# A written sequence for the closing part of a perceiver block

## The chip, the core and the metric

The kernel runs on one core of a Trainium2 chip. The core has five instruction queues: TensorE (PE, with its weight loads as PEld), VectorE (DVE), ScalarE (ACT), GpSimd (POOL) and SyncE (SP, which here only issues DMAs). Each queue runs in order, and the queues wait for each other by semaphores. The metric is the device time of one execution in microseconds (us); less is better.

## What is computed

16 items, each with x of 128 x 512 and a context of 2048 x 512, all in float32. Three stages, each added to its input, each behind a layernorm:

```python
x = x + softmax(ln(x) @ ctx.T) @ ctx                      # cross attention
q, k, v = heads of ln(x) through W*_down and W*_up        # 16 heads of 32, rotary halves
x = x + (softmax(causal(q @ k.T * scale)) @ v) @ Wc       # self attention
h = ln(x); g = softmax over the top 2 of (h[row 0] @ Wr.T)
x = x + h + sum over the two chosen experts e of g[e] * ((h @ A[e].T) @ Bw[e].T)
```

Which experts an item uses is known only when the first row of its own h is; their weights are then gathered from DRAM by index.

## The kernel before, in words

Python generators hold the stages of one item, and `step(kind, b, n)` runs n parts of a generator: `score` (L265: context scores and their softmax), `attend` (L328: the weighted context, matmuls av in four quarters, and the layernorm 2), `inner` (L350: q, k, v, heads, output projection o, and layernorm 3) and `experts` (L650: routing, the two experts' matmuls mid and ffn, result and store). The weights are folded first; then a loop (L760) takes items 0 to 13, one round each, in which item b runs `inner`, b - 1 runs `experts`, b + 1 `attend`, b + 2 `score`. From L808 on stands the closing part for items 13 (only its experts), 14 (called y) and 15 (called z), which have no later item to run beside.

The sequence of instructions comes from the compiler's scheduler, which may change the order on an engine, except between instructions that were given to `tc.keep_in_program_order` (called `pinned`, L112): these keep the order in which the program names them. All matmuls and transposes are pinned (L99, L102); on DVE and POOL only a few are, on ACT almost none.

A tile from a pool lies in a room that goes by its tag; a pool with bufs=1 has one room per tag, and a new tile in it waits until all readers of the old one are done. PSUM has eight banks: three for `ps_tr`, two for `ps_sc`, three for `ps_acc`.

Parts that the prediction follows:

- `layernorm` (L128): statistics on DVE (L132, L134), the root on POOL (L136, L139), the normalising pass on DVE (L142).
- `transposed` (L169): for most items by DVE blocks and two DMAs; where `by_tensor` holds (items 0, 1 and the last ones) by four PE transposes and an ACT copy (L178).
- `weigh` (L437): for each group of four heads a masked add (L441), a maximum (L447), four exponentials on ACT (L449), a reciprocal and a multiplication (L453, L454).
- `route` (L562): one matmul lg, seven small DVE operations, two indirect gathers into `each` (L581), one into `wb` (L586), and a POOL copy from `each` into `wa` (L591). `each` has one room.
- `early` (L608): for item 15 the first row alone is carried through v, output projection, layernorm and routing ahead of the others, so that its experts are known sooner: matmuls v0, v0t, o0 (by `padded`, L635), o0t, tr_row, with copies on DVE (L627, L635).
- `experts`: mid (L666), its scaling by the gate on ACT (L671), the residual sum `res` (L674, L676), ffn (L683), the result (L684) and the store (L685), on POOL's queue except for item 15. `res` has one room.

## Time and profile before

| | us |
|---|---|
| three runs | 838.35, 835.94, 838.13; median 838.13 |
| the profiled execution | 836.97 |
| span of its records | 835.2 |
| matmuls of item 14's first head scores begin (closing part) | 752.69 |
| last matmul ends | 829.34 |
| last DVE instruction ends | 831.50 |
| the two last stores are issued | 831.19 and 831.9 |

The page sums the busy time of each engine and cuts the span into 40 slices. A line of stretches gives, after its bounds and length, the busy time and count of PE, PEld, DVE, ACT and POOL, then the granted TensorE clock (1.00 is full), the DMA share and GB/s. A line of waits gives who stood, for whom, the sum, how often and the longest. A line of the chain gives start, length, engine and tile. The names there are those of the program: h for a layernorm's result, rs for its root, res for the residual sum, each, wa and wb for the experts' weights.

### The profile page before, as it was taken

The numbers are of one execution on the slowest core, as the hardware profiler recorded it, in microseconds if no ns is written. First come the engines' busy times: TensorE is split into PE (matmuls) and PEld (weight loads), VectorE is DVE, ScalarE is ACT, GpSimd is POOL, SyncE is SP. The second block draws the span as 40 slices with busy tenths as digits, with TensorE's granted clock in tenths as the row PEclk, the third lists the DMA queues.
The fourth block names the chain that finished last, engine by engine and source line by source line (L and its number), as shares of the span: only waits on it lengthen the run. The fifth ranks groups of instructions, "written<-read, shape, count | busy, mean of one in ns | idle before, by whom it ended". The sixth has DMA issues, their size and how long they took to land.

```text
span 835.2 us, 14284 instructions
## 1 busy us (share of the span) xinstructions
PE 804.6 (96%) x5500; PEld 569.6 (68%) x5500; DVE 529.9 (63%) x1234; ACT 258.9 (31%) x766; POOL 146.1 (17%) x215
## 2 busy tenths in 40 slices
PE   6999999999999999999999999999999999997974
PEld 6846675768677676868667576867757686864733
DVE  1454759386675849577585948667593956657652
ACT  1223324142232415133332424223241512324331
POOL 1001001212121111212111121212111121212013
PEclk9999999999999999999999999999999999999878
DMA  9998294968849495876949496785949578551002
GB/s 368 396 349 340 90 369 172 345 248 273 335 163 414 147 357 218 300 301 204 398 143 381 174 332 271 248 345 182 386 159 352 218 276 329 177 214 38 1 20 69
DMA packets 76739, 211.04 MB, mean 253 GB/s; under 512 B 6400, under 2 KB 42624, under 8 KB 60288
## 3 DMA queue, kind: packets, MB, share of 16 engines
q10 hardware_dynamic: 15696, 113.32, 33.9%
q1 hardware_dynamic: 56880, 84.23, 28.7%
q0 software_dynamic: 4096, 12.59, 4.6%
q8 instruction: 43, 0.70, 0.3%
q14 instruction: 24, 0.20, 0.1%
HBM read 180.23 MB, written 29.88 MB: 252 GB/s over the span
## 4 chain that ended last, share of the span: by engine, by line
PE 89%; DVE 5%; POOL 2%; ACT 1%; issue 1%; DMA 1%; DVEq 0%; POOLq 0%; ACTq 0%
PE psc L100 28%; PE av L100 25%; PE v L100 7%; PE o L100 6%; PE k L100 6%; PE q L100 6%; PE y L100 2%; PE pss_sc L100 2%; PE pss_acc L100 1%; PE mid L100 1%; PE ffn L100 1%; ACT att L449 1%; DMA each<-in_A_dram,g_blocks 1%; PE lg L100 0%; PE tr_m L103 0%
## 5 line engine op out<-in xcount | busy, mean ns | idle before, releaser
L100 PE MATMUL psc<-hT,ctxT 128*128 128x128 f32 x2048 | 237.3, 277 | 1.4 <-ACT hT L178 1.4
L100 PEld LDWEIGHTS psc<-hT,ctxT 128*128 128x128 f32 x2048 | 233.3, 193 | 2.5 <-ACT hT L178 2.0
L100 PE MATMUL av<-ctx,sc 128*128 128x512 f32 x512 | 227.1, 595 | 0.0
L100 PEld LDWEIGHTS av<-ctx,sc 128*128 128x128 f32 x512 | 94.5, 190 | 111.0 <-issue 108.8
L449 ACT ACTIVATE att<-att,nmx 128x128 f32<-128x128 f32 x256 | 98.7, 387 | 91.4 <-DVE nmx L447 91.4
L136 POOL TENSOR_SCALAR rs<-mv 128x1 f32<-128x1 f32 x48 | 10.8, 225 | 410.2 <-DVE g_at L575 209.3
L287 ACT COPY sc<-psc 128x512 f32<-128x512 f32 x64 | 37.5, 586 | 140.1 <-PE psc L100 140.1
L315 ACT ACTIVATE sc<-sc 128x512 f32<-128x512 f32 x64 | 40.2, 630 | 90.9 <-DVE sc L312 90.4
L100 PE MATMUL v<-w_v,hT 128*32 128x512 f32 x520 | 60.5, 605 | 0.9 <-DVE w_v L234 0.9
L100 PE MATMUL k<-hT,w_k 128*128 128x128 f32 x512 | 60.9, 277 | 0.0
L100 PE MATMUL o<-w_c,yT 128*128 128x512 f32 x128 | 59.7, 609 | 0.5 <-ACT yT L493 0.5
L100 PEld LDWEIGHTS k<-hT,w_k 128*128 128x128 f32 x512 | 59.3, 194 | 1.2 <-issue 1.2
L100 PE MATMUL q<-hT,w_q 128*128 128x128 f32 x512 | 60.0, 275 | 0.0
L100 PEld LDWEIGHTS q<-hT,w_q 128*128 128x128 f32 x512 | 58.5, 192 | 0.3 <-issue 0.3
L290 DVE TENSOR_TENSOR mx<-psc,mx 128x512 f32<-128x512 f32 x32 | 21.6, 676 | 55.6 <-ACT sc L287 55.6
L142 DVE TENSOR_SCALAR h<-x,mv,rs 128x512 f32<-128x512 f32 x48 | 28.2, 587 | 37.3 <-POOL rs L139 37.3
L415 ACT ACTIVATE kb<-kT,cst 128x512 f32<-128x512 f32 (+1 forms) x34 | 36.2, 1111 | 43.0 <-DVE kT L403 43.0
L449 ACT ACTIVATION_READ_ACCUMULATOR att<-att,nmx 128x1 f32 x256 | 47.8, 187 | 0.0
L312 DVE TENSOR_TENSOR sc<-sc,spread 128x512 f32<-128x512 f32 x64 | 42.6, 672 | 3.3 <-PE spread L100 3.3
L454 DVE TENSOR_TENSOR att<-att,rsm 128x512 f32<-128x512 f32 x64 | 43.3, 677 | 0.7
L447 DVE TENSOR_REDUCE nmx<-att 128x4 f32<-128x512 f32 x64 | 41.6, 672 | 0.0
L290 DVE TENSOR_TENSOR mx<-psc,sc 128x512 f32<-128x512 f32 x16 | 11.1, 691 | 47.2 <-ACT sc L287 47.2
(134 smaller groups left out, 855.4 us busy)
## 6 DMA issues: line engine op xcount, KB each, us to landing
ctx<-in_ctx_dram ACTq DMA_DIRECT2D x56, 1024.0 KB, 8.9
ctxT<-in_ctxT_dram ACTq DMA_DIRECT2D x52, 1024.0 KB, 10.6
there_p<-pX SPq DMA_DIRECT2D x28, 512.0 KB, 4.0
pT<-there_p SPq DMA_DIRECT2D x28, 512.0 KB, 4.5
ctxT<-in_ctxT_dram SPq DMA_DIRECT2D x12, 1024.0 KB, 8.0
there<-blocks SPq DMA_DIRECT2D x42, 256.0 KB, 3.3
hT<-there SPq DMA_DIRECT2D x42, 256.0 KB, 3.0
ctx<-in_ctx_dram SPq DMA_DIRECT2D x8, 1024.0 KB, 9.2
```

The costliest lines, as they stand in the source:

```text
L100: tc.keep_in_program_order(nc.tensor.matmul(*args, **kwargs))
L136: eps = nc.gpsimd.tensor_scalar_add(rstd, mv[:, 1:2], EPS)
L142: place(nc.vector.tensor_scalar(to, of, mv[:, 0:1], rstd, ALU.subtract, ALU.mult))
L287: nc.scalar.copy(sc[:, v], ps)
L290: nc.vector.tensor_tensor(mx, ps, mx if v > 1 else sc[:, 0], ALU.max)
L312: nc.vector.tensor_tensor(sc[:, v], sc[:, v], spread[:, None, :S].to_broadcast([P, 4, S]), ALU.add)
L315: nc.scalar.activation(sc[:, v], sc[:, v], AF.Exp)
L415: nc.scalar.activation(kb[:, chunks, half, :].rearrange("p c (q i) -> p c q i", q=4), kT[:, chunks, :].rearrange("p c (i q) -> p c q i" if ...
L447: nc.vector.tensor_reduce(nmx[:, hs], att[:, hs, :], AX.X, ALU.max, negate=True)
L449: nc.scalar.activation(att[:, i, :], att[:, i, :], AF.Exp, bias=nmx[:, i : i + 1], accum_out=sm[:, i : i + 1],)
L454: nc.vector.tensor_tensor(att[:, hs, :], att[:, hs, :], rsm[:, hs, None].to_broadcast([P, 4, S]), ALU.mult)
```

## The change

The closing part from the second quarter of `attend` for item 15 on is cut into some 150 named pieces, and a text lists them in the order in which they are issued. A name is the piece and its item: m0.14 is the masked add of head group 0 of item 14, mx the maximum, e the exponentials, n the normalising; av, den, rden, x1 are the end of `attend`; st, mv, rs, h (2, 3 or r for the row) the layernorm; tr, hT transposes and copy; k, q with S, P, C, A the four rotary steps and kb the blocked copy; pss the head scores; tp, pT transposes and copies of the probabilities; v, vv, y, yT, o, x2 the rest of `inner`; share, lg, choose, ga, gb, wa, ex, gate the routing; mid, midT, f, rx, r the experts; v0, v0s, v0t, pad, row_o, o0s, o0t, row, trr the early row.

The list as far as the second layernorm of item 15, and its end:

```diff
+CLOSING = """
+pss0.14 av1.15 m1.14 m0.14 share.13 mx1.14 rx.13 e1.14 lg.13 fold.15 av2.15 choose.13 mx0.14
+ga.13 last_fold.15 e0.14 n1.14 den.15 av3.15 ex.13 n0.14 gb.13 rden.15 gate.13 wa.13 pss1.14
+x1.15 tp0.14 st2.15 mv2.15 mid.13 m2.14 rs2.15 pT0.14 h2.15 midT.13 mx2.14 tr2.15 f.13 m3.14
+hT2.15 e2.14 k0.15 r.13 mx3.14 n2.14 e3.14 q0.15 k0S.15 k0P.15 n3.14 k1.15 q0S.15 q0C.15
+k0C.15 k0A.15 q1.15 k1C.15 kb0.15 k1S.15 k1P.15 k1A.15 tp1.14 q1C.15 kb1.15 q0P.15 v0.15
+q0A.15 pT1.14 q1S.15 pss0.15 q1P.15 v0s.15 q1A.15 v0t.15 m1.15 mx1.15 pss1.15 pad.15 m0.15
+e1.15 y.14 mx0.15 row_o.15 m2.15 yT.14 n1.15 e0.15 o.14 mx2.15 m3.15 o0s.15 mx3.15 n0.15
+e3.15 o0t.15 x2.14 tp0.15 e2.15 row.15 v.15 st3.14 pT0.15 mv3.14 n2.15 rs3.14 str.15 h3.14
+n3.15 tr3.14 mvr.15 tp1.15 hT3.14 rsr.15 vv.15 share.14 hr.15 lg.14 pT1.15 y0.15 choose.14
+trr.15 yT0.15 y1.15 share.15 ex.14 ga.14 lg.15 gate.14 yT1.15 o0.15 choose.15 gb.14 o1.15
+rx.14 ex.15 ga.15 gate.15 x2.15 st3.15 wa.14 mv3.15 rs3.15 mid.14 gb.15 h3.15 midT.14 tr3.15
+rx.15 wa.15 f.14 hT3.15 mid.15 r.14 midT.15 f0.15 f1.15 r0.15 r1.15
+"""
```

While the list runs, every instruction on DVE, ACT and POOL is kept in program order, as those on PE are:

```diff
+    class InOrder:
+        def __getattr__(self, name):
+            issue = getattr(self.engine, name)
+            def kept(*args, **kwargs):
+                ins = issue(*args, **kwargs)
+                if closing:
+                    tc.keep_in_program_order(ins)
+                return ins
+            return kept
+    vector, scalar, gpsimd = InOrder(nc.vector), InOrder(nc.scalar), InOrder(nc.gpsimd)
...
-    pinned = tc.keep_in_program_order
+    def pinned(ins):
+        if not closing:
+            tc.keep_in_program_order(ins)
```

Tiles become `Later` objects, which take their room at the first use; this holds for the rounds of items 0 to 13 too, which otherwise make the same calls in the same order through the split helpers. The copies of the early row move from DVE to ACT, tiles of item 15 take rooms of their own, and the stores of items 13 and 14 go to SP's queue:

```diff
-            nc.vector.tensor_copy(t, ps)
+            scalar.copy(t, state[name])
-        nc.vector.tensor_copy(padded[:, :, 0], tr[:, :KC])
+            pad=lambda: scalar.copy(padded[:, :, 0], state["tr"][:, :KC]),
-        each = p1.tile([P, TOP, KC * R], F32, tag="each", name=f"each_{b}")
+        each = Later(
+            p1, [P, TOP, KC * R], tag="each" if b < B - 1 else "mx", name=f"each_{b}"
+        )
+            tag = "partner" if n == "k" or chunks == every else "blocks_3"
-        res = p1.tile([P, D], F32, tag="res", name=f"res_{b}")
+        res = Later(p1, [P, D], tag="res" if b < B - 1 else "kT", name=f"res_{b}")
-            ps = bank(ps_acc, "acc", f"ffn_{b}_{at}")
+            pool, tag = (ps_sc, "sc") if b >= B - 2 else (ps_acc, "acc")
+            banks[cols.start] = bank(pool, tag, f"ffn_{b}_{cols.start}")
-            (nc.sync if b == B - 1 else nc.gpsimd).dma_start(out[b][:, cols], res[:, cols])
+            (nc.sync if b >= B - 3 else gpsimd).dma_start(out[b][:, cols], res[:, cols])
...
+    closing.append(True)
...
+    for name in CLOSING.split():
+        pieces[name]()
```

## The prediction

> **What bounds the kernel now.** I read the page's busy times and slices first, then the closing part in stretches, then what TensorE waits for there, then the chain that ended last.

> ```profile
> PE 804.6 (96%) x5500; PEld 569.6 (68%) x5500; DVE 529.9 (63%) x1234; ACT 258.9 (31%) x766; POOL 146.1 (17%) x215
> PE   6999999999999999999999999999999999997974
> PEclk9999999999999999999999999999999999999878
> ```

> TensorE (PE) is the bound, and only the last four slices of 20.9 us show gaps in it and a lower granted clock. Busy times by stretch (sum, then PE, PEld, DVE, ACT, POOL, then clock):

> ```profile
> 752.69:766.00 13.31, 12.99 (x46) 6.65 (x46) 12.09 (x34) 6.56 (x33) 0.08 (x1) 1.00 0.02 6
> 768.00:772.53 4.53, 0.00 (x1) 0.04 (x1) 0.98 (x3) 0.64 (x2) 2.65 (x5) 0.74 0.33 102
> 793.92:796.82 2.90, 0.00 (x0) 0.00 (x0) 2.29 (x6) 0.68 (x3) 0.81 (x2) 1.00 0.24 90
> 805.32:807.35 2.03, 0.00 (x0) 0.03 (x1) 1.03 (x4) 0.73 (x2) 0.78 (x2) 1.00 0.00 0
> 820.27:823.98 3.71, 0.00 (x1) 0.00 (x0) 1.50 (x3) 0.37 (x1) 1.39 (x3) 1.00 0.11 35
> ```

> Four stretches have no matmul at all. In the waits of that part, PE stood for these:

> ```profile
> PE tr L103 <- DVE h L142: 8.4, 2, 4.6
> PE o L100 <- DVE padded L635: 2.9, 1, 2.9
> PE tr_row L100 <- DVE hrow_row L142: 2.0, 1, 2.0
> ```

> The chain tells why the layernorm (h) was late, once at 771.6 and once at 823.2: its root stood on POOL behind the experts' gathers.

> ```profile
> 767.31 2.69 DMA each<-in_A_dram,g_blocks
> 770.12 0.61 POOL wa L591
> 770.73 0.21 POOL rs L136
> 771.64 0.75 DVE h L142
> ...
> 818.79 2.76 DMA each<-in_A_dram,g_blocks
> 821.67 0.61 POOL wa L591
> 822.28 0.22 POOL rs L136
> 827.06 2.42 DMA out_dram<-res
> 829.57 1.08 DVE res L676
> ```

> **The budget of before**, from pss0.14 at 752.69 to the last matmul at 829.34, is 76.65 us. PE work at full rate, by the spacing of matmuls in the timeline (0.43 us for one 512-wide pass, 0.116 for one 128-wide): av1 to av3 10.3, o of 14 and 15 6.9, v 3.4, k and q 7.4, tp 3.8, mid 2.9, f 2.6, pss 3.9, y 2.0, tr 1.4, the early row (v0, v0t, row_o, o0t, trr) 4.5, lg and den 1.1: 50.2 us. The clock, in windows of 1 us, was at half rate from 770.2 to 777.0, 797.5 to 800.9, 807.8 to 814.6 and 824.8 to 828.2; PE was busy for 4.5, 3.4, 6.8 and 3.0 of it, and half of that, 8.8 us, is lost. What is left, 17.6, is waiting: 15.4 in which PE is idle in the rows and some 2 of pipeline tails ahead of the gaps.

> The rate changes lie multiples of 3.41 us apart. The stretch 794.1 to 797.5 held 0.7 us of matmuls and 804.3 to 807.8 held 1.4, and each was followed by half rate; so I count a window used to 42% or less as one that lowers the rate of the next. [...]

> **The change, part by part.** It adds no matmul and no pass over data. I laid the pieces in the order of the list on each engine, with these durations: DVE 0.69 for 512 columns (next start after 0.60), 0.44 for 256 (0.34), choose 1.6, gate 0.6; ACT four exponentials 1.56, a 512 copy 0.59, kb 0.91; POOL root 0.9, two gathers 2.6 until the queue is free and 4.1 until landed (765.92 to 770.00), third gather 1.3, wa 0.61. A piece starts 0.07 us after its last input or when its engine is free. The same durations in the order of *before* put k0 at 775.4 (trace 775.4), o.14 at 786.7 (787.0), and the end of r1 at 833.0 (831.5): 1.5 us late in 80.

> - **Routing of 13 pulled ahead.** share.13 needs hT of 13, fetched at 750.7 and landed 2.8 us later, so it runs at 755.9, its matmul lg.13 at 757.1 behind av1. Gathers go out at 758.9 (before: 765.9) and wa.13 is done at 763.7. Now rs2.15 finds POOL free: x1 764.7, mv2 766.5, h2 768.3. PE has pss1.14, tp0.14 and mid.13 until 767.4, so tr2.15 waits 0.96 instead of 4.6, and no half rate follows. DVE is what comes next in line: rx.13 and choose.13 stand ahead of mx0, so e0 starts at 760.0, hidden by av2 and av3 (6.9 us).
> - **k, q and the scores.** k0 starts at 769.7, q1 ends at 777.1 (before 785.0). tp1.14, v0, v0t are put between, so both pss.15 find q, k and kb ready: none waits (before 0.2 and 1.2).
> - **Early row on ACT.** v0s, pad and o0s leave DVE, where pad stood behind m, h and mx (2.9 us). A pad copy on ACT isn't in the trace: between 0.16 (DVE's) and 0.59 (a 512 copy), taken 0.22; it is done at 781.3 and needed at 782.9, so both ends cost nothing. o0t comes at 787.4, trr at 795.5 (before 807.4).
> - **o.14 next to the row.** o.14 runs from 784.0 to 787.4, v covers x2.14, rs3.14 and h3.14 (787.6 to 792.1). Small waits remain ahead of o.14, lg.14, trr, y1 and lg.15: 0.2 to 0.4 each, 1.0 in sum.
> - **Tail.** o1 ends at 800.8 (before 819.4). From there the waits are new: POOL holds ga.14, gb.14 and then ga.15 until 802.6, so wa.14 ends at 803.25 and mid.14 stands 2.6 us; rs3.15, free to go at 802.6, stands behind wa.14 until 803.2; tr3.15 waits 0.75, f0 0.6. One window of little work follows o1, and I count half rate for 804.3 to 807.8: 1.5 us. gb.15 and wa.15 (806.0) are needed at 807.7.
> - **Own rooms.** each of 15 lies in the room of mx, so ga.15 need not wait for wa.14 (before 817.5 against routing ready at 813); res of 15 lies in that of kT, so rx.15 doesn't wait for the store of 14 (2.8 us on DVE before; 1.7 us at the end). The stores of 13 and 14 leave POOL for SP: 0.67 us at 793.2, ahead of rs3.14, is gone. On SP they queue ahead of the last two stores; the one of 14 goes at 808.7, its 2.4 us end by 811.1 while the last begin at 810.5: I take 0.3 us.

> Sum: 50.2 work + 5.9 waits (0.96 + 1.0 + 2.6 + 0.75 + 0.6) + 1.5 half rate = 57.6, so the last matmul ends at 810.3 and r1 at 810.8; before 831.5. That is 20.7 less, 20.4 with the stores. The profiled execution took 836.97 (span 835.2): 816.6. The median of before is 838.13, 1.2 above it; by that 817.7. I say **817**.

> **Rivals.**
> - **Half of it (824 to 835).** The fixed order makes every late piece hold all behind it on its engine. With hand-offs of 0.3 instead of 0.07 us the same lay-out ends 7.7 us later: 824.3. For: the list has some 150 pieces and waits on all engines. Against: rows show 0.02 to 0.15 us between an end and the start that it releases.
> - **DVE holds POOL (821 to 822).** The list packs DVE around the gathers. If each POOL instruction is held by one DVE pass (0.69), r1 ends 4.7 later: 821.3. Against: 32 gathers in the trace took 953, 986 and 1111 ns (least, median, most), in rounds where DVE is 63% busy. [...]
> - **It doesn't do what it says (836 to 840).** A shared room not counted, a PSUM bank for example, makes list and rooms wait for each other as before. I went through the banks of the three PSUM pools (3, 2 and 3) in the order of the list: only trr waits for one, 0.2 us.
> - **Slower: the rounds ahead of the closing part.** Every helper of the fourteen rounds is rewritten and takes kb, yT and others later. A round is 47.86 us (POOL roots at 601.39, 649.25, 697.11). If the new taking of rooms lets PE stand in each, 14 rounds eat the gain from 1.5 us a round on (20.4 / 14); at 2 us a round the time is 816.6 + 28 = 844.6. Against: the calls of a round, their order and what is pinned are the same, and PE stands at 9 tenths in every slice there.

> **How the numbers follow.** A measurement of this kernel tells some 0.3% (2.5 us) from no change. Chances: my forecast (812 to 821) 0.72; held POOL 0.08; half of it 0.11; doesn't do what it says 0.03; slower 0.06. Below my sum lie no half rate (1.5), and the lateness of the lay-out (1.5): 813.6; above it one more window of half rate over o0 and o1 (1.7), since trr, lg and y fill PE thinly ahead of them as they did from 807.8 to 811.2 with no return of the clock; held POOL 4.7; together 823. Range 812 to 824. Faster 0.91, same 0.03, slower 0.06.

> **What would show it.** tr2.15 waits about 1 us, not 4.6; no half rate before 795; o1.15 ends near 801; ga.15 follows gb.14 at once; PE stands ahead of mid.14, released by wa; rx.15 waits for no store; the span up to 752.7 is as before. Wrong would be: gathers longer than 1.1 us, waits on ACT's copies of the early row, or a start of pss0.14 that has moved.

## The result and the profile after

The changed kernel takes **815.51 us** (median of four runs, 815.0 to 816.47); the kernel before, beside it, 838.05 (median of four, 835.94 to 838.35). The ratio is 0.9738, with a 95% interval from 0.9719 to 0.9756: 22.5 us less, 2.6%. The forecast was 817, with a range of 812 to 824. The profiled execution took 815.19 us, and its records span 813.4.

The page of the kernel after, busy times and slices:

```profile
PE 797.0 (98%) x5500; PEld 564.9 (69%) x5500; DVE 529.8 (65%) x1231; ACT 259.9 (32%) x769; POOL 146.2 (18%) x213
PE   6999999999999999999999999999999999999996
PEclk9999999999999999999999999999999999999999
```

The count of matmuls is the same, 5500, and the busy times of DVE, ACT and POOL are within 1 us of before. What has changed is the end of the two rows of digits: the dents of the last four slices are gone. PE's busy time is 7.6 lower, for the most part (7.2, in the budget below) because a matmul at a lower clock counts as busy for longer.

The closing part in stretches (sum, then PE, PEld, DVE, ACT, POOL, then clock, DMA share, GB/s):

```profile
768.00:794.40 26.40, 26.03 (x213) 16.71 (x211) 22.35 (x54) 16.86 (x64) 1.84 (x4) 1.00 0.03 12
794.40:800.71 6.31, 6.31 (x52) 3.60 (x52) 5.28 (x26) 1.92 (x6) 3.65 (x4) 1.00 0.18 55
800.71:803.17 2.46, 0.01 (x1) 0.00 (x0) 2.18 (x7) 0.11 (x1) 2.11 (x3) 1.00 0.35 127
803.17:809.90 6.73, 6.27 (x26) 4.48 (x26) 2.93 (x4) 1.32 (x3) 2.99 (x4) 0.75 0.31 97
```

One of the four stretches without matmuls is left, 800.71 to 803.17, and only behind it is the clock low, 0.75. From 768.0 to 800.7 PE is busy for all but 0.4 us. The waits of PE in the kernel after, from 750 on:

```profile
PE mid L138 <- POOL wa L115: 2.5, 1, 2.5
PE tr L141 <- DVE h L115: 0.6, 1, 0.6
PE ffn L138 <- ACT mid L115: 0.5, 1, 0.5
PE lg L138 <- ACT vv L115: 0.4, 1, 0.4
```

(L138 and L141 are the helpers for matmuls and transposes now, L115 the wrapper that issues everything on DVE, ACT and POOL.) The layernorm h, which cost PE 8.4 us in two waits, costs 0.6 in one; the waits for the padded row and for hrow_row are gone. The chain that ended last shows both places:

```profile
765.77 0.19 DVE mv L115
...
766.04 0.24 POOL rs L115
...
767.76 0.66 PE tr L141 x4
...
801.55 0.95 POOL each L115
802.50 0.63 POOL wa L115
...
803.17 1.80 PE mid L138 x8
804.98 1.11 PE tr L141 x4
...
807.42 0.91 PE mid L138 x8
```

At 766.04 the root rs follows its statistics (mv) by 0.08 us; no gather stands ahead of it. From 800.7 on the chain runs over POOL's gather and copy (each, wa) to mid.14, and the length of mid tells the clock: 1.80 us for eight matmuls at 803.17, 0.91 for the same eight at 807.42.

**The budget.** I cut each trace from the first matmul of pss0.14 to the last matmul into windows of 0.5 us. Idle is what of a window PE isn't busy; loss is busy time by (1 - clock); the rest is work at full rate, with what the last matmul ahead of a gap outlasts the spacing in it (at 512 columns a row is 0.59 us long, and where a next one follows, that starts after 0.43). "End" is from the last matmul to the end of the span.

| | before | after | difference |
|---|---|---|---|
| start of pss0.14 | 752.69 | 752.14 | -0.55 |
| idle | 15.54 | 3.95 | -11.59 |
| loss to the clock | 8.89 | 1.71 | -7.18 |
| work at full rate | 52.22 | 52.10 | -0.12 |
| **pss0.14 to last matmul** | 76.65 | 57.76 | -18.89 |
| end | 5.86 | 3.50 | -2.36 |
| span | 835.2 | 813.4 | -21.8 |

The start isn't the change's: in the profiles of the twelve kernels below, whose new code is alike up to there, it lay from 751.9 to 753.8. So the experiments are read by two lengths that don't contain it: **T**, from pss0.14 to the last matmul, and the **end**. T of one and the same kernel, the one after, was 57.76 in one profile and 58.33 in another, so a difference in T of some 0.6 us decides nothing by itself.

### The profile page after: what moved, and what is told of

Read it like the earlier page. It is cut to its first block, busy times and chain, and to the rows that moved or that the text cites. A ratio compares the mean times of both kernels' runs of the same rounds, so it can differ in the third digit from the quotient of the medians.

```text
span 813.4 us, 14283 instructions
## 1 busy us (share of the span) xinstructions
PE 797.0 (98%) x5500; PEld 564.9 (69%) x5500; DVE 529.8 (65%) x1231; ACT 259.9 (32%) x769; POOL 146.2 (18%) x213
## 4 chain that ended last, share of the span: by engine, by line
PE 95%; DVE 2%; POOL 1%; issue 1%; DMA 0%; ACT 0%; POOLq 0%; DVEq 0%; ACTq 0%
PE psc L138 29%; PE av L138 27%; PE v L138 7%; PE k L138 7%; PE q L138 7%; PE o L138 6%; PE pss_sc L138 2%; PE y L138 2%; PE mid L138 2%; PE ffn L138 2%; PE pss_acc L138 2%; PE tr L141 1%; PE tr_m L141 0%; PE spread L138 0%; PE lg L138 0%
## 5 line engine op out<-in xcount | busy, mean ns | idle before, releaser
L138 PE MATMUL psc<-hT,ctxT 128*128 128x128 f32 x2048 | 237.0, 277 | 1.4 <-ACT hT L115 1.4
L138 PEld LDWEIGHTS psc<-hT,ctxT 128*128 128x128 f32 x2048 | 233.0, 193 | 2.5 <-ACT hT L115 2.0
L138 PE MATMUL av<-ctx,sc 128*128 128x512 f32 x512 | 227.3, 596 | 0.0
L138 PEld LDWEIGHTS av<-ctx,sc 128*128 128x128 f32 x512 | 94.4, 190 | 110.5 <-issue 109.5
L115 ACT ACTIVATE att<-att,nmx 128x128 f32<-128x128 f32 x256 | 98.8, 388 | 84.9 <-DVE nmx L115 84.8
L115 POOL TENSOR_SCALAR rs<-mv 128x1 f32<-128x1 f32 x48 | 10.7, 224 | 435.9 <-DVE g_at L115 209.2
L115 ACT COPY sc<-psc 128x512 f32<-128x512 f32 x64 | 37.5, 586 | 140.0 <-PE psc L138 140.0
L115 ACT ACTIVATE sc<-sc 128x512 f32<-128x512 f32 x64 | 40.2, 630 | 90.9 <-DVE sc L115 90.4
L138 PE MATMUL k<-hT,w_k 128*128 128x128 f32 x512 | 60.1, 275 | 0.0
L138 PE MATMUL q<-hT,w_q 128*128 128x128 f32 x512 | 60.0, 275 | 0.0
L138 PE MATMUL v<-w_v,hT 128*32 128x512 f32 x520 | 59.0, 593 | 0.9 <-DVE w_v L115 0.9
L138 PEld LDWEIGHTS k<-hT,w_k 128*128 128x128 f32 x512 | 58.5, 192 | 1.5 <-issue 0.8
L138 PEld LDWEIGHTS q<-hT,w_q 128*128 128x128 f32 x512 | 58.5, 192 | 0.0
L138 PE MATMUL o<-w_c,yT 128*128 128x512 f32 x128 | 57.8, 594 | 0.0
L115 DVE TENSOR_TENSOR mx<-psc,mx 128x512 f32<-128x512 f32 x32 | 21.6, 675 | 54.9 <-ACT sc L115 54.9
L115 DVE TENSOR_SCALAR h<-x,mv,rs 128x512 f32<-128x512 f32 x48 | 28.2, 587 | 33.3 <-POOL rs L115 33.3
L115 ACT ACTIVATE kb<-kT,cst 128x512 f32<-128x512 f32 (+1 forms) x34 | 36.2, 1112 | 39.7 <-DVE kT L115 39.7
L115 ACT ACTIVATION_READ_ACCUMULATOR att<-att,nmx 128x1 f32 x256 | 47.9, 187 | 0.0
L115 DVE TENSOR_TENSOR sc<-sc,spread 128x512 f32<-128x512 f32 x64 | 42.6, 672 | 3.3 <-PE spread L138 3.3
L115 DVE TENSOR_TENSOR att<-att,rsm 128x512 f32<-128x512 f32 x64 | 43.4, 678 | 0.8
L115 DVE TENSOR_REDUCE nmx<-att 128x4 f32<-128x512 f32 x64 | 41.9, 672 | 0.1
L115 DVE TENSOR_TENSOR mx<-psc,sc 128x512 f32<-128x512 f32 x16 | 11.1, 691 | 46.2 <-ACT sc L115 46.2
```

What stands on the lines that cost most here:

```text
L115: ins = issue(*args, **kwargs)
L138: tc.keep_in_program_order(nc.tensor.matmul(*args, **kwargs))
```

## The experiments

Theory **A**: the gain comes from the places of the work in the list, because PE then hardly stands for DVE or POOL until 800.7 (0.6 us, at tr2.15), and the work itself is unchanged. Rivals: **B**, holding DVE, ACT and POOL to program order, the own rooms and the moved queues do it, whatever the order; **C**, each part of the list brings its own share, and the shares add up. The gain is then taken apart: routing, rooms, queues, copies, and what is left at 800.7. Where a time stands alone it is one run; the first four ran beside a before of 835.57, the next four beside 838.57, the last four (five rounds each) beside 836.4.

**The order of before in the new code.** Everything is kept but the list:

```diff
 CLOSING = """
-pss0.14 av1.15 m1.14 m0.14 share.13 mx1.14 rx.13 e1.14 lg.13 fold.15 av2.15 choose.13 mx0.14
+pss0.14 pss1.14 fold.15 av1.15 last_fold.15 m0.14 m1.14 mx0.14 mx1.14 e0.14 m2.14 av2.15 m3.14
+e1.14 mx2.14 n0.14 mx3.14 e2.14 n1.14 den.15 share.13 e3.14 n2.14 lg.13 av3.15 n3.14 rden.15
...
```

> The changed kernel with its list put into the order that the engines showed before the change (read off the trace of before), everything else kept: pins, own rooms, copies on ACT, stores on SP. Theory A (the gain lies in which work stands at each wait): the lay-out with the same durations ends 19.2 us later than with the list as it is, so 815.5 + 19.2 = 834.7, within 2. Rival B (pins, rooms and queues carry the gain, whatever the order): 816 to 819.

It took 834.2 us. T is 76.44 (before 76.65), idle 15.40 and loss 8.74. The waits of PE in this kernel:

```profile
PE tr L141 <- DVE h L115: 7.7, 2, 4.7
PE o L138 <- ACT padded L115: 3.3, 1, 3.3
PE tr_row L138 <- DVE hrow_row L115: 2.2, 1, 2.2
```

They are those of before, with other names for the lines: h 8.4 then and 7.7 now, padded 2.9 and 3.3, hrow_row 2.0 and 2.2. So B falls: rooms, queues, ACT's copies and kept order are all in this kernel, and T has not moved. Only the end has, 3.50 instead of 5.86. T's gain of 18.9 needs the new sequence: without it all the rest brings nothing.

**New front, old rest; old front, new rest.** The first follows the list up to q1.15 and from there the order of before; the second has the order of before up to h2.15 and then the list.

```diff
+e2.14 k0.15 r.13 mx3.14 n2.14 e3.14 q0.15 k0S.15 k0P.15 n3.14 k1.15 q0S.15 q0C.15 k0C.15 k0A.15
+q1.15 tp1.14 pT1.14 y.14 yT.14 kb0.15 q0P.15 q0A.15 k1S.15 pss0.15 ...
```

> The list as it is up to and with q1.15, then all the remaining pieces in the order of before. Theory A: the front's waits are filled with work that the later waits then lack, so nearly nothing is kept; the lay-out ends 20.2 later than the whole list: 835.7, within 2.5. Rival C (the gain of 8 us that stands at the end of q1 in the comparison of both traces is kept to the end): 838.05 - 8 = 830.

```diff
+choose.13 ex.13 ga.13 tp0.14 gate.13 x1.15 pT0.14 st2.15 tp1.14 mv2.15 gb.13 pT1.14 wa.13 rs2.15
+h2.15 rx.13 mid.13 midT.13 tr2.15 f.13 hT2.15 k0.15 r.13 q0.15 k0S.15 ...
```

> The order of before up to and with h2.15 (the routing of 13 behind the weighing of all head groups of 14), then the rest of the list as it is. Theory A: the lay-out ends 2.7 to 6.1 us later by where the windows of the clock fall: 818 to 821.6. Rival C (the routing of 13 pulled ahead brings the 8 us by which q1 ends sooner): 815.5 + 8 = 823.5 or more.

With the new front alone: 832.46 us, T 74.62. It has q1.15 done at 776.9, the kernel before at 785.1; counted from pss0.14 that is a lead of 8.0, and only 2.0 of it are left at the end (T 76.65 less 74.62). PE's waits show where they went:

```profile
PE pss_acc L138 <- DVE qT L115: 3.7, 1, 3.7
PE tr L141 <- DVE h L115: 3.2, 2, 2.6
```

The waits for h (3.2), for the padded row (2.4) and for hrow_row (2.2) are still there, and two have grown: the one for qT at the second scores, 0.4 in before, is 3.7, and at the first scores PE stands 1.5 for kb. The lead of PE was given back at the next things that it needed from DVE and ACT.

With the old front: 821.65 us, T 62.56, 4.8 more than after. Here one wait carries it, and POOL's timeline tells why:

```profile
PE mid L138 <- POOL wa L115: 5.4, 2, 2.9
```

```profile
767.00 1.10 POOL L115 DMA_INDIRECT each<-in_A_dram,g_blocks  x1 [14.16 <-DVE g_row L115]
771.30 0.61 POOL L115 COPY wa<-each 128x512 f32<-128x512 f32 x1 [0.67 <-DMA each<-in_A_dram,g_blocks]
```

The experts of 13 are gathered from 767.0 on, and mid.13, now ahead of k0, waits 2.9 for wa, with half rate behind it (the loss to the clock is 3.39, in after 1.71). The other wait of the two is the one that the kernel after has too, 2.5 at mid.14. C falls: the front up to h2.15 is worth 4.8 if the rest is new, and the longer front up to q1.15, which contains it, only 2.0 if the rest is old. A lead is kept only as far as no later wait takes it back.

**The list up to o.14, then the order of before.** This cuts behind the early row's first half:

```diff
+y.14 mx0.15 row_o.15 m2.15 yT.14 n1.15 e0.15 o.14 n0.15 x2.14 st3.14 mv3.14 rs3.14 m3.15 h3.14 ...
```

> The list as it is up to and with o.14, the remaining pieces in the order of before. Theory A: the gain grows with every part whose waits are filled, and the lay-out ends 12.2 us later than with the whole list: from pss0.14 to the last matmul 70.0 (within 2), time 827.7. Rival C (what q1 has gained is kept and the rest is the tail's): 8 us kept, so 838 - 8 - 2.4 for the stores and rooms of the end = 827.6 as well in time, but with waits only ahead of the tail's pieces (tr3.15, mid) and none ahead of trr.

It took 828.82 us, T 70.99 (idle 9.91, loss 8.93):

```profile
PE o0t L138 <- ACT o0s L115: 4.1, 1, 4.1
PE tr L141 <- DVE h L115: 3.2, 2, 2.6
```

T is within 2 us of A's 70.0, and waits remain ahead of trr too (1.3 for hrow_row), where C wanted none. So of T's gain of 18.9 the list up to q1.15 brings 2.0, the list from there to o.14 3.6 more (74.62 to 70.99), and what follows o.14 the other 13.2, on condition of the two ahead of it. The greater part is in the last third. As I read the list, it is that o0s and the row's steps come ahead of the end of the weighing, and that the routing of both items sits beside y, o0 and o1; what the runs show is that no long wait, and so no half rate, comes until 800.7.

**No kept order on DVE, ACT and POOL.** The list stays; the compiler's scheduler may change the order on these three engines:

```diff
-                if closing:
+                if closing and False:
```

> The list as it is, but DVE, ACT and POOL aren't kept in program order in the closing part; only PE's order is held. Theory A: PE's order decides, and the scheduler places the others as they become ready: 815 to 819. Rival B (holding the order on the other engines is what brings the gain): 825 or more.

It took 820.73 us, T 61.79. Its waits:

```profile
PE mid L138 <- POOL wa L115: 4.0, 1, 4.0
PE tr L141 <- DVE h L115: 1.4, 2, 1.0
```

These are two waits of the kernel after, 1.5 and 0.8 us longer; yT (1.0) and g_part (0.7) follow. That is above what A allowed (815 to 819) and far from B's 825 and more: keeping the order on the three engines is worth 4.0 of the 18.9, and only with the right order to keep.

**Routing of 13 put later.** The prediction gave the 4.6 us of tr2.15 to the routing of 13. Here its pieces move back behind the weighing of groups 0 and 1:

```diff
+pss0.14 av1.15 m1.14 m0.14 mx1.14 rx.13 e1.14 fold.15 av2.15 mx0.14 last_fold.15 e0.14 n1.14
+share.13 den.15 lg.13 av3.15 n0.14 rden.15 choose.13 ga.13 ex.13 gb.13 gate.13 wa.13 pss1.14 x1.15
```

> The list as it is, with the routing of 13 alone put later: share.13 behind n1.14, lg.13 behind den.15, choose.13 to wa.13 behind rden.15, so that its gathers go out some 3.6 us later. Theory A1 (the place of the routing itself is worth little; what held it in before were the weighings of groups 2 and 3): from pss0.14 to the last matmul 58.1 to 59.2 instead of 57.8, with waits ahead of mid.13 and tr2.15 of 1.6 together; time 815.8 to 817. Rival A2 (as the prediction's step has it, the early routing is what takes the 4.6 us of wait ahead of tr2.15 away): some 4 us of wait come back, 61.5 or more; 819.5.

It took 815.33 us, T 58.12.

```profile
PE mid L138 <- issue: 2.5, 1, 2.5
PE tr L141 <- DVE h L115: 1.1, 2, 0.6
PE mid L138 <- POOL wa L115: 0.7, 1, 0.7
```

(The first line is the wait at mid.14; its releaser isn't named here, the length is the same 2.5. Of the second, 0.5 is at tr2.15 and 0.6 at tr3.15.) T is only 0.36 more than after, but the two can't be set against each other as they stand: this kernel lost nothing to the clock, and after lost 1.71. Up to the end of o1.15, where neither has half rate, it takes 49.49 us from pss0.14, and after 48.57 in both of its profiles. So the later routing costs 0.9, most of it the 0.7 at mid.13; tr2.15 stands no longer than in after, and A2's 4 us don't come back.

The gathers, though, aren't back at their old time. POOL's first one in this kernel, then in the kernel after:

```profile
761.90 1.10 POOL L115 DMA_INDIRECT each<-in_A_dram,g_blocks  x1 [10.92 <-DVE g_row L115]
```

```profile
758.47 1.10 POOL L115 DMA_INDIRECT each<-in_A_dram,g_blocks  x1 [7.29 <-DVE g_row L115]
```

Counted from pss0.14 they go out after 13.2 us in before, 10.0 here and 6.3 in after. So the place of the routing itself brings 3.6 us of their lead, and the other 3.3 are enough to free the root of item 15. For these one thing is left that the list has taken from ahead of choose.13: pss1.14, and with it the weighing of groups 2 and 3 of item 14, now come behind av3. In before the masked adds, maxima and normalising of these groups stood ahead of choose.13 on DVE, the gathers went out at 765.9 only, and the root behind them. I name this as the cause by elimination; no run moved pss1.14 alone.

This kernel shows something else: its clock stays full until 813.37, behind the last matmul. The rate changes of a trace lie multiples of 3.41 us apart, so the windows of PE can be counted back from there:

```profile
799.71:803.13 3.42, 1.71 (x4) 1.00 0.47 144
803.13:806.54 3.41, 2.01 (x13) 1.00 0.16 48
...
813.37:813.60 0.23, 0.00 (x0) 0.50 0.00 0
```

The wait is as long as in the kernel after, but it lies across two windows, used to 50% and 59%, and no half rate follows. In after one window, 800.1 to 803.5, held nearly all of it and was used to 28%.

**The room of res, and the stores.** Three kernels. The first gives res of 15 the room of res again (rx.15 then goes behind r.14); the second puts the early row's copies back on DVE and the stores of 13 and 14 on POOL; the third moves the store of 14 alone.

```diff
-        res = Later(p1, [P, D], tag="res" if b < B - 1 else "kT", name=f"res_{b}")
+        res = Later(p1, [P, D], tag="res", name=f"res_{b}")
```

> The changed kernel, but res of item 15 back in the one room of res, and rx.15 moved behind r.14, since it then has to wait for the store of 14. Theory A (the own room of res is worth the wait for the store): r.14 ends at 808.15 in the trace of after, its store lands some 2.5 later at 810.7, rx.15 (1.1) and r0 (0.45) follow: the last DVE instruction comes 2.3 us later, 817.8. Rival (the store lands anyway before the last matmuls are done, or the room is not needed): within 0.5 of 815.5. The stretch from pss0.14 to the last matmul stays 57.8 in both.

```diff
-            scalar.copy(t, state[name])
+            vector.tensor_copy(t, state[name])
-            pad=lambda: scalar.copy(padded[:, :, 0], state["tr"][:, :KC]),
+            pad=lambda: vector.tensor_copy(padded[:, :, 0], state["tr"][:, :KC]),
-            (nc.sync if b >= B - 3 else gpsimd).dma_start(out[b][:, cols], res[:, cols])
+            (nc.sync if b == B - 1 else gpsimd).dma_start(out[b][:, cols], res[:, cols])
```

> The list as it is, but v0s, pad and o0s are copied on DVE at the same places of the list, and the stores of 13 and 14 are issued on POOL again. Theory A (only places count): from pss0.14 to the last matmul 57.5 to 58.3, time within 1 of 815.5. Rival (moving work off DVE and POOL is part of the gain): 2.9 us for pad's place on DVE and 0.7 for each store, 60.5 or more, 818 or more.

```diff
-            (nc.sync if b >= B - 3 else gpsimd).dma_start(out[b][:, cols], res[:, cols])
+            (nc.sync if b in (B - 3, B - 1) else gpsimd).dma_start(out[b][:, cols], res[:, cols])
```

> The changed kernel with the store of item 14 alone on POOL's queue, as before the change. Theory A6 (a store that POOL issues late ends later than one that SP issues, and the program's end waits for it): the time from the last DVE instruction to the end of the span grows from 3.0 to some 4.5, time 1.5 more than the unaltered kernel. Rival (the 1.5 us of the run with copies and stores put back came with the copies): 3.0 and no difference.

| | time | T | end | last DVE to the end of the span |
|---|---|---|---|---|
| after, profiled | 815.19 | 57.76 | 3.50 | 3.03 |
| after, five rounds more | 816.53 (median) | 58.33 | 3.50 | 3.03 |
| res in one room | 819.04 | 58.41 | 5.26 | 3.20 |
| copies on DVE, both stores on POOL | 818.68 | 58.38 | 5.02 | 4.56 |
| store of 14 on POOL | 817.29 (median) | 57.87 | 5.16 | 4.69 |

With one room the end is 1.76 longer, as A had it (2.3 forecast) and not its rival, and DVE's timeline names the transfer that rx.15 waits for:

```profile
812.17 1.07 DVE L115 TENSOR_TENSOR res<-x,h 128x512 f32<-128x512 f32 x1 [2.15 <-DMA out_dram<-res]
```

The copies on DVE cost T nothing (58.38 against 58.33): it is their place in the list that counts, not the engine. In time that kernel meets its rival's 818 or more, but by the end alone. The store of 14 on POOL costs nothing in T either, but the end is 1.66 longer. The time goes the same way, 817.29 against 816.53 and 815.51 of after, though the intervals overlap: a ratio to before of 0.9771 (0.9756 to 0.9785) against 0.9749 (0.9733 to 0.9765). POOL and SP in that kernel:

```profile
808.79 0.61 POOL L115 DMA_DIRECT2D out_dram<-res  x1 [2.04 <-DVE res L115]
...
810.30 0.83 SPq L926 DMA_DIRECT2D out_dram<-res  x2
```

The two last stores are issued by SP from 810.30 on, as in the kernel after; the one on POOL is issued at 808.79 and lands some 2.4 us later, long before the span ends at 815.4. So the end doesn't wait for that landing; what it waits for is told in the last section.

**The kernel after again, and its last wait filled.** The first is the kernel after, unaltered, for comparison. The second adds two 512-wide matmuls behind o1.15, whose result nobody reads: work added. The third adds them ahead of tr3.15 and moves wa.14 ahead of ga.15, so that mid.14 and f.14 come earlier.

> The changed kernel once more, unaltered, as the measure for the three others of this group. All theories: 815.5 within 1; from pss0.14 to the last matmul 57.8 with half rate in the tail, or 56.1 to 56.6 without, by where the 3.41 us windows of the clock fall.

```diff
+        def fill():
+            ps = bank(ps_tr, "tr", f"fill_{b}")
+            for _ in range(2):
+                matmul(ps, ident, w["c"][:, 0, :], start=True, stop=True)
...
-lg.15 gate.14 yT1.15 o0.15 choose.15 gb.14 o1.15 rx.14 ex.15 ...
+lg.15 gate.14 yT1.15 o0.15 choose.15 gb.14 o1.15 fill.15 rx.14 ex.15 ...
```

> The changed kernel with two matmuls of 512 columns behind o1.15 whose result nobody reads; they fill 1.7 of the 2.5 us in which PE waits for wa.14. Theory A4 (the tail's 1.7 us of loss is the clock's answer to that wait): no half rate, tr3.15 and f.14 at full rate, 0.7 to 1.4 us from pss0.14 to the last matmul less than a run with half rate; ratio to the unaltered kernel 0.9985. Rival (the rate falls for another reason, or the tail hangs on POOL alone): no difference, or later by what the matmuls take.

```diff
+lg.15 gate.14 yT1.15 o0.15 choose.15 gb.14 wa.14 o1.15 rx.14 ex.15 ga.15 gate.15 x2.15 st3.15
+mv3.15 rs3.15 mid.14 midT.14 gb.15 h3.15 f.14 fill.15 tr3.15 rx.15 wa.15 hT3.15 mid.15 r.14
```

> The same two matmuls, and wa.14 ahead of ga.15 on POOL, f.14 ahead of tr3.15 on PE, so that PE works while item 15's layernorm is made. Theory A5: PE no longer waits 2.5 us for wa.14 but that much longer for h3.15, which is the tail's chain; from pss0.14 to the last matmul 0.7 to 1.4 less than the unaltered kernel with half rate, no better than the fill alone by more than 0.3. Rival (POOL's order costs the 2.5 us of wait): 2 us or more less.

| five rounds | median | ratio to before, 95% interval | T | idle | loss |
|---|---|---|---|---|---|
| after again | 816.53 | 0.9749 (0.9733 to 0.9765) | 58.33 | 4.48 | 1.56 |
| filled | 814.74 | 0.9743 (0.9728 to 0.9758) | 57.18 | 3.10 | 0.00 |
| filled, and mid.14 early | 815.65 | 0.9750 (0.9734 to 0.9766) | 57.45 | 3.20 | 0.00 |

PE in the filled kernel:

```profile
800.51 1.88 PE L138 MATMUL fill<-w_c,ident 128*128 128x512 f32 x4
803.13 1.16 PE L138 MATMUL mid<-hT,wa 128*128 128x128 f32 x8 [0.74 <-POOL wa L115]
805.01 0.63 PE L141 MATMUL tr<-ident,h 128*128 128x128 f32 x4 [0.72 <-DVE h L115]
```

The half rate is gone: mid.14 takes 1.16 instead of 1.80 and tr3.15 0.63 instead of 1.11. In the filled kernel the windows of the clock lie as in after (pss0.14 starts at 752.1 in both, and the clock falls at 813.7 in both, behind the work), and the one that was used to 28% is now used to 78%; so it is the added work that kept the rate, and not another lie of the windows. But tr3.15 now stands 0.72 for h, which in after's first profile mid.14 at half rate covered, so of the 1.6 to 1.7 of loss, 0.6 to 1.1 of T is won. (In after again half rate comes 1.2 us later against the work, from 805.8, behind mid.14. tr3.15 stands 0.63 for h there, about what its T is longer by.) The intervals of the times overlap; whether the fill makes a faster kernel isn't decided. Moving wa.14 ahead of ga.15 brings nothing beyond it.

## Why the prediction was right

- **Work.** 50.2 was forecast and 52.1 measured; 52.2 in before too. The change adds no work, as said; but 2 us of it I had counted as waiting in before, as pipeline tails ahead of the gaps. The rows show only 0.16 of that at a gap (0.59 against 0.43), 0.6 at four; and three of the four gaps have gone and the 2 us have not. By the starts of the pieces in after they are spread over many of them: av1 to av3 take 10.7 (10.3 counted), o 7.3 (6.9), the early row 4.9 (4.5), pss 4.3 (3.9).
- **Waits.** Of 5.9 forecast, 3.95 came: mid.14 2.46 (2.6 forecast), tr2.15 0.57 (0.96), f0 0.46 (0.6), the small ones together 0.46 (1.0), tr3.15 none (0.75; mid.14 at half rate covered it). The two misses, 1.9 too little work and 1.95 too much waiting, cancel: T was forecast as 57.6 and is 57.76. That it fits to 0.2 is luck; the sum is better than its terms.
- **Clock.** 1.5 forecast from 804.3 to 807.8, 1.71 measured. Windows of PE of the kernel after:

```profile
803.00:804.00 1.00, 0.83 (x5) 0.75 0.49 131
804.00:805.00 1.00, 1.00 (x6) 0.50 0.00 0
```

  The 3.4 us ahead of it, 800.1 to 803.5, held 0.95 us of matmuls, 28%, and half rate followed, as it had in before behind four windows used to 21% to 41%. With 1.9 us of matmuls in the gap (78%) none followed. That the gap fell into one window was luck too: in the kernel with the routing put later it did not, and no half rate came.
- **Routing of 13 pulled ahead.** The effect came: the gathers go out at 758.47 (forecast 758.9), and tr2.15 waits 0.57 instead of 4.6. The cause was named in part only. The place of the routing is worth 0.9 us, and without it tr2.15 waits no longer. What else held the gathers back in before, by elimination the weighing of groups 2 and 3 of item 14, the step doesn't name.
- **k, q, the early row, o.14.** k0 starts at 769.12 (forecast 769.7), q1 ends at 776.51 (777.1), o1 at 800.71 (800.8). ACT's pad took 0.17 (0.22 taken). But that these copies leave DVE, which the step gave as the reason, is not what took the 2.9 us of pad away: with the copies back on DVE, at the same places of the list, T is unchanged.
- **Own rooms and queues.** That of res is worth 1.76 (1.7 forecast). That of each is worth nothing that shows: the kernel that puts wa.14 ahead of ga.15 (and f.14 ahead of tr3.15) has T 57.45, against 57.18 with the fill alone. The stores were mis-sized, with the wrong sign: I took 0.3 us of cost for the queue on SP; from the last DVE instruction to the end it went from 3.70 to 3.03, and with the store of 14 back on POOL to 4.69. This and r1 (810.37, forecast 810.8) make the profiled execution 1.4 us shorter than the 816.6 of the sum.
- **The rivals.** The rounds are as before: POOL's roots stand at 600.53, 648.39 and 696.25, 47.86 apart. Hand-offs grew nowhere: k0, q1 and o1 came when 0.07 us each had them. The list and its rooms do what they say. DVE holding POOL is there in kind, but small, below: no run shows the whole pass of 0.69 from which the rival's 4.7 is counted, the rows show 0.2 to 0.45 on a few POOL instructions. By the prediction's own words gathers longer than 1.1 us would have been a sign of being wrong, and there are some of 1.19 to 1.39.

## What to carry to other kernels

In an end without other items to run beside, a lead is kept only if no later wait takes it back: the front of this list was worth 2.0 us with the old rest and 4.8 with the new one, so such a sequence is to be laid out whole, to the last matmul. Ask of each wait which passes of the slow engine stand ahead of the late piece, and not which engine is named as its releaser; and test the named cause, since an effect that comes as forecast doesn't prove it. Long waits cost twice where the clock follows them: here 11.6 us of idle went, and 7.2 of half rate with them. And look at what each queue issues last: a late store on POOL cost 1.7 us that no matmul and no pass shows.

## What the runs showed of the hardware

**DVE and POOL.** Against a DVE pass that holds POOL the prediction set the 32 gathers of before (953 to 1111 ns). None of those lay beside a pass of the kind that goes with longer ones in after: the only DVE passes over two wide tiles beside gathers of before, x<-av,x at 766.59 and x<-o,x at 819.42, read one of the two, av or o, from PSUM. In the kernel after gathers lie beside passes over two SBUF tiles (att<-att,rsm at 759.58 and 761.19, res<-x,h at 799.35 and 804.96). POOL, then DVE:

```profile
789.86 0.85 POOL L115 TENSOR_TENSOR rs<-rs,mhalf 128x1 f32<-128x1 f32 x1
...
804.34 1.39 POOL L115 DMA_INDIRECT wb<-in_BT_dram,g_rows  x1 [0.19 <-DMA each<-in_A_dram,g_blocks]
805.74 0.80 POOL L115 COPY wa<-each 128x512 f32<-128x512 f32 x1
```

```profile
789.57 0.72 DVE L115 TENSOR_TENSOR att<-att,rsm 128x512 f32<-128x512 f32 x1
...
799.35 1.07 DVE L115 TENSOR_TENSOR res<-x,h 128x512 f32<-128x512 f32 x1
...
804.96 1.10 DVE L115 TENSOR_TENSOR res<-x,h 128x512 f32<-128x512 f32 x1
```

The root's last step takes 0.85 beside a DVE pass that reads two SBUF tiles (0.56 to 0.58 usually), the copy wa 0.80 beside another (0.61), gathers 1.25, 1.28 and 1.39 (0.94 to 0.99). The gather at 801.55, beside x<-o,x with its PSUM input, takes 0.95, and so does the one at 798.80, which has res<-x,h beside it in its last 0.4 us only. So these POOL instructions took 0.2 to 0.45 us longer beside such a pass, not a whole pass. DVE shows nothing of the kind: res<-x,h of items 14 and 15 takes 1.07 and 1.10 here, and 1.12 and 1.07 in before (L676, at 796.68 and 829.57), where no POOL instruction lies beside it. All but one of these POOL rows are off the path that sets the end; the gather at 800.06, 1.19 long where its like take 1.06 to 1.11, stands ahead of wa.14.

**The end of the program.** With the store of 14 issued by POOL, 1.5 us ahead of the last ones, the span ends 1.66 us later after the last matmul, although that store lands first. The last rows of the program (L1123) hold a DRAIN on each queue, after which the queues meet by semaphores. The kernel after, then the one with the store on POOL (how many; shortest, median and longest in ns; first and last start):

```profile
L1123 POOLq DRAIN  x3: 46/97/7327, 804.4 to 813.1; - x3
L1123 SPq DRAIN  x3: 7/7/7, 812.6 to 812.9; - x3
```

```profile
L1123 POOLq EVENT_SEMAPHORE  x4: 17/17/17, 814.7 to 815.3; - x4
L1123 POOLq DRAIN  x3: 46/97/5860, 808.8 to 815.1; - x3
L1123 SPq DRAIN  x3: 7/7/7, 813.0 to 814.9; - x3
```

The long DRAIN of POOL, the first of its three, ends at 811.7 in the kernel after, ahead of SP's first at 812.6. With the store it ends at 814.6, when SP's has been over since 813.0, and POOL's semaphores follow it at 814.7. In both this DRAIN ends 5.2 to 5.3 us after the end of POOL's last instruction (806.54 to 811.7, 809.40 to 814.6), and in before too (827.73 to 833.0). So what holds the end there is POOL's DRAIN, and in these kernels a last instruction of POOL is late when it ends less than some 5 us before SP is through. In before POOL's DRAIN ended at 833.0 and SP's at 834.4; the step from 3.70 to 3.03 between the last DVE instruction and the end has another cause, which stays open.
